# A gated cross-attention block: output projection by seven products over two head pairs, and a build-time planner for every queue

## The chip, the cores and the metric

The kernel runs on one core of a Trainium2 chip. A core has TensorE (PE in the profile; PEld is its loading of stationary operands), VectorE (DVE), ScalarE (ACT), GpSimd (POOL) and SyncE (SP), each with a queue of its own that it works off in order, and 16 DMA engines. Working memory is SBUF; matmul results go to PSUM, of which eight banks of 128 x 512 fp32 are used. The metric is device time in microseconds, the median of the runs.

## The reference

32 sequences of 64 tokens, width 512. With LN a layer norm without scale:

```
q = LN(x) Wq ; k = ctx Wk ; v = ctx Wv            32 heads of 128
P = softmax(q k^T / sqrt(128) + bias), keys masked per sequence
x1 = x + tanh(g0) * (P v) Wo
out = x1 + tanh(g1) * (LN(x1) W^T + b + LoRA(LN(x1)))   LoRA by sequence
```

All is fp32. Bias is 32 x 32 x 64 x 64, Wq, Wk, Wv are 512 x 4096, Wo is 4096 x 512, the last linear layer 512 x 512.

## The kernel before, in words

The tokens go through in two halves (`NPH` = 2) of 1024, eight tiles of 128 tokens (two sequences) each. Heads go in 16 pairs.

**Precision.** Large matmuls are split: an operand is rounded to a high part (`ACT` copy to `fp32r`) and a low part (a subtraction on DVE or POOL), and `mm3` (L93) issues high x high, high x low and low x high, three matmuls for one. Scores and values are plain fp32 matmuls of 64 columns (`ps` L862, `po` L1015).

**Seven products.** Keys, queries and values are made block by block, 2 x 2 blocks, by Strassen's scheme in Winograd's form: seven products instead of eight, from sums of weight blocks (`pair_blocks` L262, `weight_steps` L221) and of activation blocks (`sum_blocks` L149, `turned_blocks` L198). `unit` (L348) issues the seven and adds the results up on DVE (L350). Only the first two key pairs are done plainly, so that work starts early.

**Stages of one half.** Keys of 16 pairs, stored to memory (`kd`); values in four groups of eight heads, stored (`vd`); then attention, pair by pair: queries, scores, softmax, values, output projection. Layer norm of x is computed on rows and spread to columns through a small memory tile (`lnd`, `ln`). After both halves come the linear layer and LoRA (`ffn_chunk` L1339).

**Softmax.** For each head, DVE adds scores and bias (L864) and takes the row maximum (L866); POOL subtracts it (L867); ACT takes the exponential, 512 columns at once (L876); DVE sums rows (L886) and inverts; POOL multiplies (L889). For the value matmul the probabilities are needed keys by queries: DVE transposes 32 x 32 blocks (L900), and eight ACT copies of 32 x 256 (`copy` L894, L897) put the blocks into place in `pt`.

**Output projection.** `pv` (L1000) makes the context of a pair, features by tokens, split to `ch` and `cl` (L1019, L1020). `oproj` (L1063) multiplies each 128-token tile of it, as stationary operand, with that pair's rows of Wo, in six matmuls (two heads, three each) into `pa`, and DVE adds `pa` to the accumulator `acc` (L1068), which holds x and gets x1, tokens by features. `prep_o` (L1033) loads and splits the rows of Wo, in each half anew.

**What sets the order.** Instructions are issued by hand-written code. Side work is written as generators in a list `streams`; `beat` (L63) advances each by one step after each product, and `drain` finishes one. PSUM comes from one pool of eight rotating buffers.

**The end.** `ffn_turn` (L1292) normalizes and transposes a row tile of the second half and stores it to `xtd`; `ffn_load` (L1276) reads it back features by tokens in pieces of 128 bytes; `ffn_out` (L1319) makes the 16 output tiles. The first half's tiles are turned much earlier (`acc_turned` L681).

## Time and profile before

| | |
|---|---|
| median of 3 runs | 1475.67 us (1473.54 to 1477.26) |
| span of the profiled execution | 1476.7 us |
| matmul records / PE busy | 12006 / 1467.8 us |
| DVE, ACT, POOL busy | 945.4, 714.3, 1047.3 us |
| memory traffic | 259.38 MB, mean 176 GB/s |
| transfers on the SP queue | q1, 50.7% of the 16 DMA engines' time |

The profile is of one execution, whose span is the time between its first and its last instruction; no other time of that execution is given. A busy share is an average over stages. A line names the engine, the operation, the tile written and those read, the shape, the count, busy time and mean length; behind the second bar stands the idle time just before, and what ended it. Matmul records overlap, so the time of a matmul is read from how many of them fill a stretch. An fp32 matmul leaves two records.

### The profile page before, as it was taken

To read this page: it belongs to the slowest core of one execution; us is meant where nothing else is said; L and a number is where in the kernel's file an instruction comes from. 1 tells how busy PE (TensorE), PEld (TensorE's weight loads), DVE (VectorE), ACT (ScalarE), POOL (GpSimd) and SP (SyncE) were. 2 spreads that over 40 slices of the span, in tenths; PEclk is the share of its full clock that TensorE was granted. 3 is DMA by queue.
4 is the path that set the end of the run, shared out by engine and by line. 5 is a ranking of instruction groups with operands and counts; after the bars stand their busy time and mean duration, and the time that the engine had idled before them with its cause. 6 is when DMAs were issued, how large, how long until landed. Compare 5 with 4: busy or idle time off the path is not lost.

```text
span 1476.7 us, 31286 instructions
## 1 busy us (share of the span) xinstructions
PE 1467.8 (99%) x12006; PEld 1220.8 (83%) x12006; DVE 945.4 (64%) x1592; ACT 714.3 (48%) x1582; POOL 1047.3 (71%) x1156
## 2 busy tenths in 40 slices
PE   9999999999999999999999999999999999999999
PEld 7888888888888888887788888888888888888887
DVE  5675465367776677676479756435777567757774
ACT  5444233346645565566334423334655665466611
POOL 3999378969767576766989937897885767577520
PEclk9999999999999999999999999999999999999999
DMA  5754554375444355352385765446545254625554
GB/s 201 288 202 166 181 174 168 143 273 179 157 158 133 140 188 199 114 188 94 114 290 205 247 228 185 167 143 242 187 158 186 94 180 158 228 88 180 144 128 130
DMA packets 148344, 259.38 MB, mean 176 GB/s; under 512 B 44418, under 2 KB 78210, under 8 KB 144099
## 3 DMA queue, kind: packets, MB, share of 16 engines
q1 hardware_dynamic: 147906, 256.87, 50.7%
q8 instruction: 94, 1.54, 0.4%
q10 hardware_dynamic: 288, 0.52, 0.1%
q14 instruction: 56, 0.45, 0.1%
HBM read 179.74 MB, written 77.61 MB: 174 GB/s over the span
## 4 chain that ended last, share of the span: by engine, by line
PE 93%; POOL 3%; DMA 1%; issue 1%; DVE 1%; ACT 0%; POOLq 0%; DVEq 0%; ACTq 0%
PE pa L99 21%; PE pzv L99 6%; PE pvv L99 6%; PE pxv L99 6%; PE pxq L99 6%; PE pvk L99 5%; PE pzk L99 5%; PE pxk L99 5%; PE pvq L99 5%; PE pzq L99 5%; PE po L1015 4%; PE ps L862 4%; PE pf L99 3%; PE pyv L99 3%; PE pyk L99 3%; PE pyq L99 3%
## 5 line engine op out<-in xcount | busy, mean ns | idle before, releaser
L99 PE MATMUL pa<-wo,ch 128*128 128x512 f32 x896 | 278.9, 392 | 1.2 <-POOL sm L867 1.0
L897 ACT COPY pt<-tp 32x256 f32<-32x256 f32 x452 | 182.5, 404 | 68.9 <-DVE tp L900 59.6
L99 PEld LDWEIGHTS pa<-wo,ch 128*128 128x128 f32 x896 | 166.8, 188 | 37.4 <-POOL sm L867 1.3
L99 PE MATMUL pa<-wo,cl 128*128 128x512 f32 x448 | 174.1, 389 | 0.0
L1068 DVE TENSOR_TENSOR acc<-pa,acc 128x512 f32<-128x512 f32 x192 | 129.4, 681 | 53.5 <-PE pa L99 53.5
L816 POOL TENSOR_TENSOR sm<-sm,madd 128x512 f32<-128x512 f32 x60 | 77.1, 1293 | 89.0 <-DMA sm<-bias 88.7
L889 POOL TENSOR_TENSOR sm<-sm,r 128x512 f32<-128x512 f32 x64 | 66.8, 1044 | 73.0 <-DVE r L888 66.6
L350 DVE TENSOR_TENSOR vt<-pvv,vt 128x512 f32<-128x512 f32 x64 | 44.2, 691 | 100.6 <-PE pvv L99 100.6
L1020 DVE TENSOR_TENSOR cl<-po,ch 128x512 fp32r<-128x512 f32 x112 | 74.5, 689 | 50.1 <-ACT ch L1019 49.7
L99 PEld LDWEIGHTS pa<-wo,cl 128*128 128x128 f32 x448 | 84.1, 188 | 17.5
L867 POOL TENSOR_TENSOR sm<-sm,mx 128x512 f32<-128x512 f32 x64 | 66.9, 1048 | 41.2 <-DVE mx L866 41.2
L350 DVE TENSOR_TENSOR qT<-pvq,qT 128x512 f32<-128x512 f32 x64 | 44.1, 690 | 62.4 <-PE pvq L99 60.8
L372 ACT COPY vt<-pxv 128x512 f32<-128x512 f32 x32 | 18.8, 588 | 129.9 <-PE pxv L99 129.9
L876 ACT ACTIVATE sm<-sm 128x512 f32<-128x512 f32 x62 | 39.2, 633 | 77.4 <-POOL sm L867 77.4
L350 DVE TENSOR_TENSOR kT<-pvk,kT 128x512 f32<-128x512 f32 x60 | 41.1, 685 | 52.9 <-PE pvk L99 52.3
L90 POOL TENSOR_TENSOR wo<-rawo,wo 128x512 fp32r<-128x512 f32 x56 | 71.4, 1295 | 5.0 <-ACT wo L89 5.0
L1015 PEld LDWEIGHTS po<-pt,v 64*64 64x64 f32 x3840 | 59.6, 135 | 13.0 <-issue 11.4
L1019 ACT CAST ch<-po 128x512 fp32r<-128x512 f32 x112 | 62.9, 593 | 12.0 <-PE po L1015 11.9
L1015 PE MATMUL po<-pt,v 64*64 64x64 f32 x3840 | 64.0, 220 | 2.1 <-issue 1.7
L350 DVE TENSOR_TENSOR vt<-pzv,vt 128x512 f32<-128x512 f32 x64 | 44.2, 691 | 33.2 <-PE pzv L99 32.5
L862 PE MATMUL ps<-kB,qT 128*64 128x64 f32 x2048 | 65.0, 223 | 0.5 <-issue 0.4
L862 PEld LDWEIGHTS ps<-kB,qT 128*64 128x64 f32 x2048 | 62.0, 138 | 3.9 <-issue 2.2
(999 smaller groups left out, 3866.5 us busy)
## 6 DMA issues: line engine op xcount, KB each, us to landing
kd<-kT SPq DMA_DIRECT2D x64, 512.0 KB, 3.8
vd<-vt SPq DMA_DIRECT2D x128, 256.0 KB, 2.4
kB<-kd SPq DMA_DIRECT2D x32, 1024.0 KB, 10.2
v<-vd SPq DMA_DIRECT2D x32, 1024.0 KB, 8.0
rawq<-wq SPq DMA_DIRECT2D x32, 512.0 KB, 3.7
sm<-bias SPq DMA_DIRECT2D x64, 256.0 KB, 4.8
rawo<-wo SPq DMA_DIRECT2D x32, 512.0 KB, 3.7
rawk<-wk SPq DMA_DIRECT2D x31, 512.0 KB, 5.6
```

What stands on the lines that cost most here:

```text
L90: eng.tensor_tensor(lo, raw, hi.bitcast(F32), ALU.subtract)
L99: nc.tensor.matmul(ps, a, b, start=start and i == 0, stop=stop and i == len(todo) - 1, skip_group_check=True)
L350: nc.vector.tensor_tensor(o, ps, i, ALU.add)
L816: nc.gpsimd.tensor_tensor(t, t, masks[p][0], ALU.add)
L862: nc.tensor.matmul(ps[h * S:(h + 1) * S, t, :], qT[:, i, tok], kT[:, i, tok], start=True, stop=True)
L867: nc.gpsimd.tensor_tensor(s, s, mx.unsqueeze(2).to_broadcast([P, NT, S]), ALU.subtract)
L889: nc.gpsimd.tensor_tensor(t, t, r.unsqueeze(2).to_broadcast([P, NT, S]), ALU.mult)
L897: f(pts[n == NPR - 2][dst, i, :, qi * 32:(qi + 1) * 32], of[src, :, ki * 32:(ki + 1) * 32])
L1015: nc.tensor.matmul(ps[h][d:d + S, k, :], v[keys, t, i * P + d:i * P + d + S], pt[keys, i, t, :], start=True, stop=True)
L1019: nc.scalar.copy(o, ps[h])
L1020: nc.vector.tensor_tensor(l, ps[h], o.bitcast(F32), ALU.subtract)
L1068: nc.vector.tensor_tensor(acc[t], ps, acc[t], ALU.add)
```

## The change

The file is rewritten around a planner; the tiling into two halves, 16 pairs, and seven products for keys, queries and values stays.

1. *Planner.* Code no longer issues instructions; it records operations (`Plan.add`) with the engines that may run them, an assumed duration on each, and the tiles read and written. PE's operations keep the recorded order and carry the due times. [...] SBUF is cut into pages (41 of 4 KB, 26 of 2 KB per partition, and small ones) handed out at plan time; PSUM banks are named by the code. The instructions are then issued in the order of planned start.
2. *Output projection.* Wo's rows are formed once, in the first half's key and value stages (`out_forms`): four sums and seven splits per pair, stored to memory (`fd`), and read again for each half (`out_step`). The context of two heads in even and odd sequences gives the four blocks b11 to b22, from which `values` makes seven forms. A group of two pairs takes seven products by two column blocks, each of six matmuls with the Wo form as stationary operand. The accumulator becomes features by tokens.
3. *Softmax.* The negated scores are kept, DVE takes the row minimum, and ACT does the subtraction, exponential and row sum by eight activations of 64 columns, each with a bias by row. POOL's subtraction and DVE's row sum go. The eight copies per head become eight transfers per pair from `tp` to `pt`.
4. *Layer norm of x1 and the end.* Since `acc` is features by tokens, `turned` transposes it and stores it (`xbd`), `row_tile` reads rows in pieces of 128 bytes, and mean and deviation are spread back over columns. In the second half this stands between the last output product and the linear layer, beside the first half's eight tiles.
5. The token order within a half is even sequences, then odd ones; inputs and output are laid out accordingly.

Instructions, before and after: SP transfers 663 and 1557; POOL sums 256 wide 662 and 449, 512 wide 454 and 432; DVE sums 256 wide 28 and 417, 512 wide 942 and 904; split matmuls 512 wide 5810 and 5618.

```diff
-ORDER = ("p1", "p6", "p7", "p5", "p2", "p4", "p3")
+ORDER = ("p1", "p2", "p6", "p5", "p7", "p3", "p4")
+LAYER = {"p1": 0, "p2": 1, "p6": 0, "p5": 1, "p7": 0, "p3": 1, "p4": 0}
+MM = 0.2267
+PAGES = {"F4": 41, "F2": 26, "S": 30}
+CAPS = {"f": 10, "rk": 3, "rq": 3, "ro": 1, "fo": 4, "xs": 4, "xr": 4}
+LEAD = {"SP": 6.0, "ACTQ": 6.0}
+AHEAD = 45.0
...
+    def weight(o, s):
+        e, d = min(o.engs.items(), key=lambda x: x[1])
+        if e == "PE":
+            return d + 0.25
+        if e in ("SP", "ACTQ"):
+            return 2.2 + o.bytes / 2e5 + LEAD[e]
+        return d * 1.25 + 0.25
...
+                        o = None
+                        for c in sorted(ready[e], key=lambda o: (o.ls, o.n)):
+                            if c.port and e in ("DVE", "POOL") and port > now + 1e-9:
+                                continue
+                            if e == "DVE" and "POOL" in c.engs and c.ls > now + 12.0:
+                                continue
+                            if c.alloc and not can(c):
+                                continue
+                            o = c
+                            break
+                        if o is None:
+                            break
+                    self.start(o, e, now, free, pend, allocated, ready, kinds, short)
...
+def t_act(n):
+    return 0.218 + n * 0.000735
+def t_dve(n):
+    return 0.155 + n * 0.001042
+def t_pool(n):
+    return 0.185 + n * 0.002164
...
+    def unit(w, a, sl, dst, banks, nm):
+        A, B = {}, {}
+        def step(q):
+            first = q in ("p1", "p2", "p5")
+            if q == "p1":
+                A["t"] = bank(banks[0], f"pa{nm}")
+            if q in ("p2", "p5"):
+                B["t"] = bank(banks[1 if q == "p2" else -1], f"pb{nm}{q}")
+            ps = (B if LAYER[q] else A)["t"]
+            if sl is None:
+                terms = [(w[q][kt], a[q][kt]) for kt in range(2)]
+            else:
+                terms = [(tuple(b.then(lambda t: t[:, sl]) for b in a[q][kt]), w[q][kt]) for kt in range(2)]
+            product(ps, terms, first)
+            p = ps.at()
+            if q in ("p1", "p6", "p5", "p4"):
+                copy(dst[{"p1": (0, 0), "p6": (0, 1), "p5": (1, 1), "p4": (1, 0)}[q]], p, 512)
+            else:
+                d = dst[{"p2": (0, 0), "p7": (1, 1), "p3": (0, 1)}[q]]
+                tt(VEC, d, p, d, ALU.add, 512)
+        return [lambda q=q: step(q) for q in ORDER]
...
+    def out_forms(n):
+        late = pl.t_pe + 25.0
+        raw = page("F4", [P, 1024], F32, f"ro{n}")
+        dma(raw.at(), dwo.at(lambda t: t[n]), P * 4096, late=late - 15)
+        a11, a21, a12, a22 = [raw.at(lambda t, i=i: t[:, i * 256:(i + 1) * 256]) for i in range(4)]
+        forms = sums4((a11, a12, a21, a22), f"o{n}", late)
+        for k, q in enumerate(ORDER):
+            t = page("F2", [P, 2, 2, P], F32R, f"fo{n}{q}", 2)
+            jb = lambda v: v.rearrange("p (j b) -> p j b", j=2)
+            split(forms[q].then(jb), t.at(lambda t: t[:, :, 0, :], 0), t.at(lambda t: t[:, :, 1, :], 1), 256, late=late)
+            for j in range(2):
+                dma(fd[n // 2][j * 7 + k].at(lambda t: t[:, n % 2, :], n % 2),
+                    t.at(lambda t, j=j: t[:, j].rearrange("p h b -> p (h b)").bitcast(F32)), P * 1024, late=late)
...
-        def copy(f, n, i, of, h, qi, ki):
-            src = slice(h * 64 + qi * 32, h * 64 + qi * 32 + 32)
-            dst = slice(h * 64 + ki * 32, h * 64 + ki * 32 + 32)
-            f(pts[n == NPR - 2][dst, i, :, qi * 32:(qi + 1) * 32], of[src, :, ki * 32:(ki + 1) * 32])
+    def score(a, n, banks):
+        p = a.p
...
+            mn = page("S", [P, NT], F32, f"mn{p}_{n}_{i}")
+            pl.add({"DVE": 0.7}, [sa], [mn.at()],
+                   lambda e, s=s, mn=mn: e.tensor_reduce(mn.t, s.t.rearrange("p k t c -> p t k c"), AX.XY, ALU.min))
+            r = page("S", [P, NT], F32, f"r{p}_{n}_{i}")
+            def ex(e, s=s, mn=mn, r=r):
+                for t in range(NT):
+                    v = s.t[:, :, t, :]
+                    e.activation(v, v, AF.Exp, bias=mn.t[:, t:t + 1], scale=-1.0, accum_out=r.t[:, t:t + 1])
+            pl.add({"ACT": 2.2}, [sa, mn.at()], [sa, r.at()], ex)
+            def norm(e, r=r):
+                e.reciprocal(r.t, r.t)
+                e.tensor_tensor(r.t, r.t, rv.t, ALU.mult)
+            pl.add({"DVE": 0.36}, [r.at(), rv.at()], [r.at()], norm)
+            pl.add({"POOL": 1.05, "DVE": t_dve(512)}, [sa, r.at()], [sa],
+                   lambda e, s=s, r=r: e.tensor_tensor(s.t, s.t, r.t.unsqueeze(1).unsqueeze(3).to_broadcast([P, 2, NT, 32]), ALU.mult), port=True)
+            pl.add({"DVE": 0.7}, [sa], [tp.at(None, i)],
+                   lambda e, s=s, i=i: e.transpose(tp.t[:, :, i, :], s.t.rearrange("p k t c -> p k (t c)")))
+        pt = page("F4", [P, 2, 2, 256], F32, f"pt{p}_{n}", 8)
+        a.pt[n] = pt
+        for h in range(2):
+            for qi in range(2):
+                for ki in range(2):
+                    src, dst = [slice(h * 64 + b * 32, h * 64 + b * 32 + 32) for b in (qi, ki)]
+                    dma(pt.at(lambda t, d=dst, qi=qi: t[d, qi].rearrange("p i c -> p (i c)"), h * 4 + qi * 2 + ki),
+                        tp.at(lambda t, s=src, ki=ki: t[s, ki].rearrange("p i c -> p (i c)")), 65536)
...
+        flat = lambda t: t.rearrange("p t s -> p (t s)")
+        b11, b12, b21, b22 = [ps[i][h].at(flat) for i in range(2) for h in range(2)]
+        g = {}
+        nm = f"g{p}_{n}"
+        def form(q, src, engs):
+            t = page("F4", [P, 2, 512], F32R, f"{nm}{q}", 2)
+            hi, lo = t.at(lambda t: t[:, 0], 0), t.at(lambda t: t[:, 1], 1)
+            split(src, hi, lo, 512, engs)
+            g[q] = (hi, lo)
+        def temp(k):
+            return page("F2", [P, 512], F32, f"{nm}{k}").at()
+        form("p1", b11, VEC)
+        c12 = temp("c")
+        copy(c12, b12, 512)
+        t1, t2, t3, t4 = [temp(f"t{k}") for k in (1, 2, 3, 4)]
+        tt(VEC, t1, c12, b11, ALU.subtract, 512)
+        form("p2", b21, VEC)
+        tt(VEC, t2, b22, t1, ALU.subtract, 512)
+        form("p6", t2, BOTH)
+        form("p5", t1, BOTH)
+        tt(VEC, t3, b22, c12, ALU.subtract, 512)
+        form("p7", t3, BOTH)
+        form("p3", b22, VEC)
+        tt(VEC, t4, b21, t2, ALU.subtract, 512)
+        form("p4", t4, BOTH)
+        a.g[n] = g
...
-        def o_terms(n, t):
-            h, lo = ctx_of(n)
-            w = b["o", n]
-            sl = slice(t * P, (t + 1) * P)
-            return [((h[:, i, sl], lo[:, i, sl]),
-                     (w[:, 0, i * 512:(i + 1) * 512], w[:, 1, i * 512:(i + 1) * 512])) for i in heads_of(n)]
-        def oproj(n, ts=range(NT)):
-            drain(ob.get(n))
-            for t in ts:
-                ps = psum(f"pa{p}_{n}_{t}")
-                mm3(ps, o_terms(n, t), last=(2, 5) if n == 0 and t == 0 else ())
-                nc.vector.tensor_tensor(acc[t], ps, acc[t], ALU.add)
-                beat()
+    def out_step(a, m, j, k, banks, last=False):
+        q = ORDER[k]
+        t = page("F2", [P, 2, 2, P], F32, f"f{a.p}_{m}_{j}{q}")
+        dma(t.at(lambda t: t.rearrange("p n h b -> p (n h b)")),
+            fd[m // 2][j * 7 + k].at(lambda t: t.rearrange("p n c -> p (n c)")), P * 2048)
+        terms = [(tuple(t.at(lambda t, n=n, hl=hl: t[:, n, hl, :].bitcast(F32R)) for hl in range(2)), a.g[m + n][q]) for n in range(2)]
+        key = "A" if not LAYER[q] else "B"
+        if q in ("p1", "p2", "p5"):
+            a.ps[key, j] = bank(banks[LAYER[q]], f"pc{a.p}_{m}_{j}{q}")
+        ps = a.ps[key, j]
+        product(ps, terms, q in ("p1", "p2", "p5"))
+        d = a.acc[{"p1": (0, 0), "p2": (0, 0), "p6": (0, 1), "p5": (1, 1), "p7": (1, 1), "p3": (0, 1), "p4": (1, 0)}[q]][j]
+        tt(VEC, d, ps.at(), d, ALU.add, 512)
...
+        for c in range(2, NPR // 2):
+            us = query_unit(a, 2 * c, xq, qb(0)) 
+            later = lambda: query_unit(a, 2 * c + 1, xq, qb(1))
+            os = out_steps(a, 2 * c - 4)
+            us[0]()
+            us[1]()
+            for k in range(14):
+                os[k]()
+                if k + 2 == 7:
+                    us += later()
+                if k + 2 < 14:
+                    us[k + 2]()
+                if k == 1:
+                    score(a, 2 * c - 1, sb(1))
+                if k == 7:
+                    score(a, 2 * c, sb(0))
+                if k == 10:
+                    values(a, 2 * c - 2, B4)
+            values(a, 2 * c - 1, B4)
+        after_q()
+        os = out_steps(a, NPR - 4, True)
+        score(a, NPR - 1, (0, 1))
+        for k in range(14):
+            os[k]()
+            if k == 7:
+                values(a, NPR - 2, B4)
+        values(a, NPR - 1, B4)
+        finish()
...
+    def turned(a):
+        for h in (1, 0):
+            for i in range(2):
+                for j in range(2):
+                    ft = 2 * i + j
+                    v = a.acc[i, h][j]
+                    t = page("F2", [P, 512], F32, f"xt{a.p}_{ft}{h}")
+                    pl.add({"DVE": 0.7}, [v], [t.at()], lambda e, v=v, t=t: e.transpose(t.t, v()), late=pl.t_pe + 5.0)
+                    dma(xbd[a.p].at(lambda d, ft=ft, h=h: d[h, ft], h * KT + ft), t.at(), P * 2048, late=pl.t_pe + 8.0)
+                    if a.p == 0:
+                        dma(xtd.at(lambda d, ft=ft, h=h: d[h, ft], h * KT + ft), v, P * 2048, late=pl.t_pe + 8.0)
+    def row_tile(p, t):
+        h, u = t // 4, t % 4
+        b = page("F2", [P, D], F32, f"{'xr' if p == 0 else 'xz'}_{t}", 4)
+        for c in range(4):
+            dma(b.at(lambda v, c=c: v[c * 32:(c + 1) * 32].rearrange("p (f k) -> p f k", k=32), c),
+                xbd[p].at(lambda d, c=c: d[h].rearrange("f (a q) w -> q (f a) w", a=4)[:, :, (4 * u + c) * 32:(4 * u + c + 1) * 32],
+                          *range(h * KT, (h + 1) * KT)), 32 * 2048, ("SP", "ACTQ")[c % 2] if p else "SP", late=pl.t_pe + t)
+        return b.at()
+    def row_moments(p, h):
+        n = NT // 2
+        mv = page("S", [P, n, 2], F32, f"mvr{p}{h}", n)
+        rows = []
+        for u in range(n):
+            t = h * n + u
+            r = row_tile(p, t)
+            moments(r, mv, u, f"r{p}_{t}", None if p else pl.t_pe + 20.0)
+            rows.append(r)
+            if p == 0:
+                dma(x1d.at(lambda d, t=t: d[t], t), r, P * 2048, late=pl.t_pe + 40.0)
+        return rows, spread(mv, deviation(mv, n, f"r{p}{h}"), n, f"r{p}{h}")[0]
...
+                turned(a)
+                made = {h: row_moments(1, h) for h in (1, 0)}
+                for t in range(NT):
+                    tile0(t)
+                for h in (1, 0):
+                    rows, spr = made[h]
+                    src1 = [a.acc[kt // 2, h][kt % 2] for kt in range(KT)]
+                    normalize([src1], [spr])
+                    act = ffn_act(1, h, src1)
+                    low = ffn_low(1, h, act, h)
+                    for u in range(4):
+                        t = h * 4 + u
+                        ffn_tile(1, t, act, low, rows[u], 4 + u if t != 3 else 2, 2 if t == 3 else 1)
...
+    seq = pl.schedule()
+    for o in seq:
+        for b in o.alloc:
+            if b.cls in PAGES:
+                b.t = pool.tile(b.shape, b.dt, tag=f"{b.slot[0]}_{b.slot[1]}", name=b.name)
+            elif b.cls:
+                b.t = psp.tile(b.shape, b.dt, tag=b.cls, name=b.name)
+        o.emit(ENG[o.eng])
```

## The prediction

> **What bounds the kernel now.** I read the busy shares first. TensorE (PE) has a matmul in flight for 99% of the span, at full granted clock.
>
> ```profile
> span 1476.7 us, 31286 instructions
> PE 1467.8 (99%) x12006; PEld 1220.8 (83%) x12006; DVE 945.4 (64%) x1592; ACT 714.3 (48%) x1582; POOL 1047.3 (71%) x1156
> ...
> PEclk9999999999999999999999999999999999999999
> ```
>
> Second, the chain that ended last, by engine and line, and then in order of time (start, length, what). It is PE nearly throughout, and the output projection `pa` is its largest item.
>
> ```profile
> PE 93%; POOL 3%; DMA 1%; issue 1%; DVE 1%; ACT 0%; POOLq 0%; DVEq 0%; ACTq 0%
> ```
> ```profile
> 359.23 2.02 PE po L1015 x128
> 361.25 1.59 PE pxq L99 x6
> 362.84 1.36 PE pyq L99 x6
> ...
> 371.00 3.88 PE ps L862 x128
> 374.88 11.11 PE pa L99 x48
> ...
> 407.28 10.88 PE pa L99 x48
> ```
>
> A 512-wide split-precision matmul costs 10.88/48 = 0.2267 us. The first group after an fp32 block (`ps`, `po`) costs 0.23 us more: 11.11 against 10.88, 1.59 against 1.36. These are the durations that matter, as matmul records of 390 ns overlap.
>
> Third, the groups of instructions, for prices (busy, mean ns, then idle before).
>
> ```profile
> L897 ACT COPY pt<-tp 32x256 f32<-32x256 f32 x452 | 182.5, 404 | 68.9 <-DVE tp L900 59.6
> L1068 DVE TENSOR_TENSOR acc<-pa,acc 128x512 f32<-128x512 f32 x192 | 129.4, 681 | 53.5 <-PE pa L99 53.5
> L867 POOL TENSOR_TENSOR sm<-sm,mx 128x512 f32<-128x512 f32 x64 | 66.9, 1048 | 41.2 <-DVE mx L866 41.2
> L1019 ACT CAST ch<-po 128x512 fp32r<-128x512 f32 x112 | 62.9, 593 | 12.0 <-PE po L1015 11.9
> L876 ACT ACTIVATE sm<-sm 128x512 f32<-128x512 f32 x62 | 39.2, 633 | 77.4 <-POOL sm L867 77.4
> ```
>
> Fourth, DVE in order of time in the second key stage: where POOL runs a sum of two SBUF tiles, DVE's own two-tile sum takes 1.25 us instead of 0.69. The two engines take turns. Back to back, a 512-wide DVE operation starts every 0.61 us; POOL's start every 0.70 us (256 wide).
>
> ```profile
> 777.38 0.69 DVE L350 TENSOR_TENSOR kT<-pzk,kT 128x512 f32<-128x512 f32 x1
> 777.99 0.16 DVE L117 TENSOR_SCALAR yx<-vx 128x8 int32<-128x8 int32 x1
> 778.06 1.25 DVE L186 TENSOR_TENSOR vs<-wvr_0b,vs 128x512 f32<-128x512 f32 x1
> ```
>
> Fifth, the first key and value stages by window (busy PE, PEld, DVE, ACT, POOL, then clock, DMA share, GB/s), and the transfers.
>
> ```profile
> 33.00:166.00 133.00, 133.00 (x589) 110.12 (x587) 78.47 (x128) 55.15 (x132) 110.41 (x143) 1.00 0.59 209
> 166.00:320.00 154.00, 154.00 (x681) 127.53 (x680) 78.85 (x117) 53.66 (x101) 124.53 (x103) 1.00 0.51 180
> ```
> ```profile
> xt<-xtd SPq DMA_DIRECT2D x64, 64.0 KB, 2.4
> ...
> ln<-lnd SPq DMA_DIRECT2D x8, 256.0 KB, 3.7
> ```
> ```profile
> 1383.37 9.64 SPq L1281 DMA_DIRECT2D xt<-xtd  x16
> ```
>
> **The change part by part.** The sum is made against the profiled span, 1476.7 us; the runs' median, 1475.67, lies 1.0 lower, inside the runs' spread.
>
> *Products.* Before: 2 halves x 16 pairs x 8 tiles x 6 = 1536 matmuls. After: 16 groups of two pairs x 7 products x 2 column blocks x 6 = 1344. 192 fewer at 0.2267 = -43.5 us, all on the bound engine. [...]
>
> *More changes between fp32 and split matmuls.* Scores and values now stand singly between products. Counted in the instruction orders, split matmuls follow an fp32 block 62 times, before 40. 22 x 0.22 = +4.8 (bounds 0, if it hides, and 5.1).
>
> *ACT.* Gone: 484 block copies x 0.404 = -196 and 64 exponentials x 0.633 = -41. Added: 512 exponentials 64 wide, with a bias by row and a row sum. No such row exists; between the 256- and 512-wide copies the slope is 0.74 ns per element, so 0.264 each at least, and I bound it above by the 256-wide copy, 0.404: +135 to +207; I take 0.27, the length being nearest to the extrapolation. Context forms: 256 copies instead of 128, +76; output-weight forms about +6. ACT then has some 695 to 767 us, about half the span: no bound. [...]
>
> *DVE and POOL in total.* By the instruction orders DVE gains 389 sums of 256 (0.413) and loses 64 row sums (0.673), 28 small transposes (0.432) and 38 sums of 512: 945+161-43-12-26 = about 1025 us. POOL loses 213 of 256 (0.75) and 22 of 512: about 874. Neither is a bound on average.
>
> *The shared turn of DVE and POOL, first key and value stages.* To the 14x11 sums of 256 for key weights and 88 of 512 for value weights come 16x11 of 256 for the output forms. All on POOL that is 330x0.70 + 88x1.25 = 341 us, and PE has 287: DVE must take a part, at 0.35 and 0.61, in turn with POOL. Along the new instruction order, priced so, the two together have 268 us of two-tile work in the 272 us of matmul from 30 us on: 98%. Before, these stages had POOL 235 of 287. With the remainders so near the limit, PE will wait here and there. Bounds: 0 (DVE takes more) and 20 (the ends of seven stretches of 40 us each late by 3). I take +4, nearest to before, where 100 us at such a share cost PE nothing.
>
> *Value blocks and their banks.* All value blocks now use the same four PSUM banks, and within an iteration the second follows the first after four products, 5.4 us, plus 1.0 for its first head. To free the banks DVE does seven 512-wide forms and one or two `acc` additions, 8.5 x 0.61 = 5.2, after the first copy (0.59) and some 0.25 of signalling at each end: 6.3 to 7.3 against 6.4. Fourteen such places: 0 to 21, and I take 0.35 each, +5. Before, eight rotating buffers hid this.
>
> *Probabilities by transfers.* 8 copies per head go; 8 transfers of 64 KB per pair come (256), on SP. From score to probabilities: 0.68+0.69+2.2+0.4+1.05+0.69 per head, two heads partly overlapped, 8 x 0.36 of issue and 2.4 to land: about 14 us. The nearest value block lies 12 products of 2.7 us behind its score: 33. Cost nothing; the cover must shrink by 19 to show.
>
> *SP and DMA.* SP issues 1557 transfers instead of 663, at 0.33 to 0.37 (0.60 for 128-byte pieces): about 570 us, below half. Traffic, counted: 258 to 363 MB. The page has 50.7% of the DMA engines for 259 MB; the mean becomes about 72%. In the first key and value stages: 209x133 + 180x154 = 55.5 MB, plus 16 output weights (8.4) and 224 forms written (29.4) = 93.3 MB. By before's share (2.83 us per MB) that is 264 of 287 us. Close, but covered: 0; end of range +35, as a rival below.
>
> *The tail.* The accumulators now hold features by tokens, so layer norm of the second half needs a turn through memory. Its cover: 8 first-half tiles x 14 x 0.2267 = 25.4, plus the last two products, 2.7: 28.1. The path: addition 0.94, transpose 0.70, store 2.75, eight gathers per queue 4.8 and landing 2.4, statistics 0.86, fifteen small operations 3.0, store 2.1, read back 4.05, eight normalizing sums and four remainders 12x0.61 + 0.5 = 7.8, and signals between some twenty steps 3: 32.4. DVE also does first-half evictions and the other group's statistics between, some 5. 37 - 28 = +9. Bounds: 0 (POOL shares the sums and queues run ahead) and 18 (gathers land twice as late). Before, PE ran through this stage without a break, so it is all new.
>
> Sum: 1476.7 - 43.5 + 4.8 + 4 + 5 + 9 = 1456.0, on the scale of the median 1455.
>
> **The rivals.**
> - *All covered.* Turns, banks and tail hide: 1476.7 - 43.5 + 4.8 - 1 = 1437. For it: ACT, DVE and POOL have room on average. Against: the tail's path has no row that would shorten it.
> - *DMA sets the first stages' pace (slower).* The forms' 128 KB writes stand in the queue ahead of weights that PE needs. The best slice of the page moved 290 GB/s; at that pace 93.3 MB take 322 us, 35 more than PE: 1490. It decides from 303 GB/s down, where the 21 us of gain are gone. For it: 92% share. Against: half of the forms are needed only much later and can wait.
> - *Value blocks wait for banks by more.* At 1.5 us in each of fourteen places: 1455 + 16 = 1471, no change. For it: DVE executes in order, and an `acc` addition that waits for its product holds the forms behind it. Against: the order was laid out with durations that the rows bear out (0.69, 1.29, 0.2267).
>
> That the products stay as many is excluded by the instruction order (5618 wide matmuls for 5810).
>
> **How the numbers follow.** Forecast case, 1445 to 1470: 0.52. All covered or better, below 1445: 0.23. Banks or tail at their upper ends, 1471 to 1480: 0.08. DMA pace or an order that does not hold on the chip, above: 0.17. Range 1437 (all covered) to 1484 (half of the DMA case). No-change means within 0.3%, about 4.4 us, what this measurement can tell. Faster 0.75, same 0.08, slower 0.17.
>
> **What would show it.** Right: matmul groups of 0.2267 as before, PE idle 15 to 25 us more, half of it before the second half's `pt` near the end. Wrong by the turns: PE waiting for POOL or DVE forms of weights before 320 us. Wrong by banks: `po` waiting for DVE. Wrong by DMA: key or value weights waiting for `wk`, `wv`, at a DMA share of 0.9. The whole fails if order and chip drift apart: then PE waits everywhere, a little each time.

## The result, and the profile after

The changed kernel takes 1564.66 us (median of four runs, 1558.32 to 1566.69) beside 1476.47 of the kernel before in the same comparison: ratio 1.0595, 95% interval 1.0569 to 1.0621. It is 88 us slower, 81 us above the end of my range.

The page of after: span, busy time by engine, the granted clock in 40 slices, and the shares of the chain that ended last.

```profile
span 1564.9 us, 33409 instructions
PE 1477.3 (94%) x11814; PEld 1199.7 (77%) x11814; DVE 1055.6 (67%) x1857; ACT 822.0 (53%) x2422; POOL 903.5 (58%) x891
PEclk9999999999999999999999999999999999999998
PE 67%; DMA 15%; DVE 5%; issue 4%; ACT 4%; POOL 3%; SPq 2%; ACTq 0%; DVEq 0%; POOLq 0%
```

PE is idle for 88 us (1564.9 - 1477.3; before: 9), and the chain, which was 93% PE, now passes through transfers for 15% of the span. No engine is full: DVE, ACT and POOL have a third to a half free. So PE does not wait for a full engine; it waits in many places for something late. The clock adds to it: the records have 13 windows at half clock, 68 us in all. PE was busy for 55 us of them, which at half rate is a loss of some 28 us, an estimate from these two numbers. Before, there was no such window.

The chain in order of time, in the second attention stage (start, length, what):

```profile
1305.35 8.70 DMA rq<-wq
...
1314.43 0.41 ACT wq_12p L352
...
1315.98 1.51 ACT sm L739 x9
1317.49 0.48 ACT qT L352
...
1318.02 2.93 PE pbq_11p L377 x6
1320.94 3.09 PE po L776 x128
```

PE at the same place, with its idle time and what ended it in brackets:

```profile
1318.02 2.93 PE L377 MATMUL pbq_11p<-q1p,wq_11p 128*128 128x512 f32 x6 [4.24 <-ACT qT L352]
```

This is the pattern of the attention stages. The raw query weights of a later pair (`rq`) take 8.70 us from issue to landing. ScalarE stands in its queue at their cast (`wq_12p`), behind it come an exponential block and then the copy `qT` that empties a PSUM bank (below, such a copy or addition is called an eviction). PE waits 4.24 us for that copy, and its next six matmuls take 2.93 us instead of 1.36: the clock has been halved. The same picture stands at 472, 1252 and 1358 us, and at 1200 us with a transfer `pt<-tp` of 6.88 us named in the load's place.

What SP issues just then (start, length, operation, count):

```profile
1305.35 0.42 SPq L366 DMA_DIRECT2D rq<-wq  x1
1307.18 7.40 SPq L366 DMA_DIRECT2D pt<-tp  x8
1314.68 0.53 SPq L366 DMA_DIRECT2D kB<-kd  x1
```

Eight placing transfers (`pt<-tp`, which put the probabilities into place) keep SP for 7.4 us; the next keys (`kB`) stand behind them. Some 4.5 us of that are the eight issues, 0.51 to 0.60 us each. The longest gaps are waits for one of the eight semaphores that tell of landings, of which each transfer needs one: the seventh was issued 0.02 us after the landing that freed its semaphore, and the eighth, at 1314.07, 0.02 us after the landing of `rq` itself. And the exponentials, in the groups:

```profile
L739 ACT ACTIVATE sm<-sm,mn 128x64 f32<-128x64 f32 x512 | 170.6, 335 | 50.2 <-DVE mn L733 46.3
L739 ACT ACTIVATION_READ_ACCUMULATOR sm<-sm,mn 128x1 f32 x512 | 96.2, 188 | 0.0
```

Each one is two instructions, and on ScalarE one exponential starts every 0.33 us: 2.65 us per head. The planner assumed 2.2, and I had 8 x 0.27.

The windows of the first key stage, the first value stage and the second value stage (length, then busy time of PE, PEld, DVE, ACT, POOL, clock, DMA share, GB/s):

```profile
27.80:164.10 136.30, 134.90 (x590) 109.91 (x589) 97.44 (x166) 85.00 (x211) 101.77 (x121) 1.00 0.91 305
164.10:333.40 169.30, 157.97 (x673) 127.14 (x671) 102.87 (x196) 83.89 (x177) 108.61 (x84) 0.98 0.89 290
...
914.10:1067.20 153.10, 153.10 (x673) 126.20 (x672) 58.79 (x91) 70.12 (x129) 136.83 (x114) 1.00 0.62 199
```

The two value stages have the same 673 matmul records; the first, which makes output-weight forms beside them, is 16 us longer.

All later readings go by stages, from the first product of a stage to the first of the next, read from the matmul records (us). "Linear" goes from the first product of the linear layer's low-rank part to the end of the last matmul. The head of a column is the number of the run, as told below. Each run but 1, 2 and 9 was planned anew with its edit, so that its order of instructions differs too.

| stage | after | 3 | 4 | 7 | 9 | 10 | 11 | 13 | 17 |
|---|---|---|---|---|---|---|---|---|---|
| keys 1 | 136.3 | 135.0 | 134.0 | 134.6 | 134.3 | 133.7 | 133.7 | 134.3 | 135.0 |
| values 1 | 169.4 | 168.7 | 170.1 | 167.6 | 168.7 | 152.3 | 158.9 | 168.6 | 152.6 |
| attention 1 | 394.0 | 370.9 | 378.0 | 370.9 | 388.4 | 391.8 | 368.0 | 378.2 | 379.9 |
| keys 2 | 186.7 | 191.6 | 175.5 | 179.8 | 186.8 | 189.8 | 178.1 | 178.2 | 178.0 |
| values 2 | 153.2 | 153.5 | 153.3 | 152.9 | 153.2 | 152.3 | 152.3 | 153.5 | 153.9 |
| attention 2 | 398.1 | 363.7 | 375.0 | 368.0 | 386.6 | 397.7 | 361.5 | 366.8 | 366.0 |
| linear | 96.3 | 94.5 | 95.0 | 91.2 | 94.2 | 93.5 | 78.0 | 90.7 | 88.0 |
| median of the runs | 1564.7 | 1510.3 | 1516.1 | 1496.9 | 1541.5 | 1542.5 | 1464.8 | 1498.2 | 1486.7 |

### The profile page after: what moved, and what is told of

Read it like the earlier page. It is cut to its first block, busy times and chain, and to the rows that moved or that the text cites. A ratio compares the mean times of both kernels' runs of the same rounds, so it can differ in the third digit from the quotient of the medians.

```text
span 1564.9 us, 33409 instructions
## 1 busy us (share of the span) xinstructions
PE 1477.3 (94%) x11814; PEld 1199.7 (77%) x11814; DVE 1055.6 (67%) x1857; ACT 822.0 (53%) x2422; POOL 903.5 (58%) x891
## 4 chain that ended last, share of the span: by engine, by line
PE 67%; DMA 15%; DVE 5%; issue 4%; ACT 4%; POOL 3%; SPq 2%; ACTq 0%; DVEq 0%; POOLq 0%
PE paq L377 9%; PE pc_0p L377 8%; PE pc_1p L377 7%; PE pak L377 7%; PE pav L377 7%; PE po L776 4%; PE ps L727 3%; DMA rq<-wq 2%; ACT sm L739 2%; SPq L366 2%; DMA vd<-vt 2%; PE pbv_0p L377 1%; PE pf L377 1%; PE pbv_1p L377 1%; PE pbv_3p L377 1%
## 5 line engine op out<-in xcount | busy, mean ns | idle before, releaser
L739 ACT ACTIVATE sm<-sm,mn 128x64 f32<-128x64 f32 x512 | 170.6, 335 | 50.2 <-DVE mn L733 46.3
L739 ACT ACTIVATION_READ_ACCUMULATOR sm<-sm,mn 128x1 f32 x512 | 96.2, 188 | 0.0
L352 ACT COPY qT<-paq 128x512 f32<-128x512 f32 x96 | 55.5, 582 | 65.2 <-PE paq L377 64.5
L352 ACT COPY vt<-pav 128x512 f32<-128x512 f32 x96 | 55.5, 586 | 57.5 <-PE pav L377 31.1
L357 DVE TENSOR_TENSOR acc<-pc_1p,acc 128x512 f32<-128x512 f32 x112 | 75.3, 678 | 6.7 <-PE pc_1p L377 6.5
L357 DVE TENSOR_TENSOR acc<-pc_0p,acc 128x512 f32<-128x512 f32 x112 | 75.4, 674 | 2.8 <-PE pc_0p L377 2.7
L357 DVE TENSOR_TENSOR kT<-pak,kT 128x512 f32<-128x512 f32 x30 | 20.6, 685 | 83.1 <-PE pak L377 66.8
L352 ACT COPY kT<-pak 128x512 f32<-128x512 f32 x90 | 52.4, 584 | 37.2 <-PE pak L377 29.0
L719 POOL TENSOR_TENSOR sm<-sm,mf 128x512 f32<-128x512 f32 x40 | 53.2, 1342 | 31.8 <-DMA sm<-bias 21.0
L749 DVE STREAM_TRANSPOSE tp<-sm 128x512 f32<-128x512 f32 x64 | 44.1, 698 | 20.8 <-PE ps L727 14.1
L377 PE MATMUL pf<-wf,fa 128*128 128x512 f32 (+1 forms) x204 | 47.9, 384 | 2.5 <-DVE ot L1012 2.5
```

Source lines behind the costliest of these rows:

```text
L352: pl.add({"ACT": t_act(n)}, [i], [o], lambda e: e.copy(o(), i()), late=late)
L357: lambda e: e.tensor_tensor(o(), a(), b().bitcast(F32) if cast else b(), f), port="POOL" in engs or engs == ("SDVE",), late=late)
L377: nc.tensor.matmul(ps, a(), b(), start=start and i == 0, stop=i == len(todo) - 1, skip_group_check=True)
L719: lambda e, s=s: e.tensor_tensor(s.t, s.t, mf.t, ALU.add), port=True)
L739: e.activation(v, v, AF.Exp, bias=mn.t[:, t:t + 1], scale=-1.0, accum_out=r.t[:, t:t + 1])
L749: lambda e, s=s, i=i: e.transpose(tp.t[:, :, i, :], s.t.rearrange("p k t c -> p k (t c)")))
```

## The experiments

In the code of the edits below, `...` and `..` stand for lines and arguments that are not shown.

### Runs 1 to 4: bytes, exponentials, number of transfers, order

Theories: A, too many bytes, so loads land late; B, the exponentials are too long; C, too many transfers; D, only the planner's numbers are off.

**Run 1**, a quarter of the bytes of every form, same transfers and order:

```diff
-dma(fd[..][:, n % 2, :], t[:, j], ...)        # P * 1024 bytes
+dma(fd[..][:, n % 2, 0:64], t[:, j, 0, 0:64], ...)
-dma(t, fd[m // 2][j * 7 + k], P * 2048)
+dma(t[:, 0, 0, :], fd[m // 2][j * 7 + k][:, :, 0:64], P * 2048)
```

> Edit: of every output-weight form only a quarter is stored and read back (64 instead of 256 columns per row and form), and the product reads that quarter four times. The number of transfers, all pages, all other instructions and the planned order stay as they are; 66 of 364 MB go, which at 71.5% of 1564.9 us for 360 MB (3.1 us of all 16 DMA engines per MB) is some 205 us of DMA time. The output projection's numbers are therefore not the reference's. Theory A (loads land later than the order assumes, because the DMA engines have too much to carry; PE then waits behind ScalarE's queue, and its clock is cut after the wait): most of the loss goes, about half of the 87.6 us of PE idle time and half of the 34 us that the cut clock costs, so 1565 - 60 = 1505 (1480 to 1525). Theory B (ScalarE's exponentials are longer than planned) and theory C (the number of transfers on SP, not their bytes): 1550 or more.

Measured: 1536.7 us, 28 less. A asked for 60. Removing 66 of 364 MB leaves more than two thirds of the loss; these bytes are a part, not the whole cause.

**Run 2**, one exponential per head:

```diff
-for t in range(NT):
-    e.activation(v, v, AF.Exp, bias=mn.t[:, t:t + 1], scale=-1.0, accum_out=r.t[:, t:t + 1])
+e.activation(s.t, s.t, AF.Exp, bias=mn.t[:, 0:1], scale=-1.0)
+e.copy(r.t, mn.t)
```

> Edit: one exponential of 512 columns per head instead of eight of 64 with a row sum each; the row minimum of the first tile stands in for all eight, and the minima stand in for the row sums, so the softmax's numbers are not the reference's. The planned order stays (the planner is still told 2.2 us). ScalarE's part of a head falls from 2.65 us (eight starts 0.33 apart) to about 0.8, 64 x 1.85 = 118 us of its 822. Theory B (exponentials take 2.65 instead of 2.2, evictions queue behind them): 1510 to 1530. Theory A (late loads): ScalarE's waits for loads stay, 1545 or more. Theory C: 1550 or more.

Measured: 1542.9 us, 22 less, at 116 us less of ACT. Between B and A: the length of the exponentials counts although ACT was only 53% busy. That it does so because they stand ahead of evictions is read from the chain above; no run moves the evictions alone.

**Run 3**, one placing transfer per pair:

```diff
-for h, qi, ki in ...: dma(pt[d, qi], tp[s, ki], 65536)
+dma(pt, tp, 524288)
```

> Edit: the probabilities of a pair go from tp to pt in one transfer of 128 rows instead of eight of 32 rows (no block is put in another place, so the values' numbers are not the reference's). Same bytes; 224 transfers fewer, and SP has 224 x 0.6 = 134 us less to issue; order planned anew with that. Theory C (SP's queue: 0.59 us for each of these issues, and issues that stand until one of eight transfers in flight has landed, 268 of 1581 in the profile): 1500 to 1520. Theory A (bytes): 1545 or more. Theory B: 1555 or more.

Measured: 1510.3 us, 54 less. The attention stages fall by 23 and 34 us, the second key stage grows by 5, the others stay within 2. It is the largest gain of one edit, and inside theory C's range. The order was planned anew, so the 54 us are the transfers' and the new order's together.

**Run 4**, three planner numbers:

```diff
-pl.add({"ACT": 2.2}, ...)            ; SP issue 0.36                    ; o.end = dma + 0.4
+pl.add({"ACT": 2.75}, ...)           ; SP issue 0.44, 0.62 for 64 KB    ; o.end = dma + 1.4
```

> Edit: three numbers of the planner alone, after the profile: exponentials 2.75 us per head (2.2), issue on SP 0.44 us and 0.62 for a 64 KB transfer (0.36), and each landing 1.0 us later. The chip has the same instructions in another order. Theory D (only the order is wrong, the engines could do it): 1490 to 1510. Theory A: loads can't be had sooner in the stages where the DMA engines are at 0.86 to 0.99, only the in-order waits of ScalarE in the attention stages go: 1525 to 1550.

Measured: 1516.1 us, 48.5 less, with the work of the kernel kept (47 operations move from POOL to DVE) and its whole output computed: between D and A, nearer to D. Attention falls by 16 and 23 us, the second key stage by 11. So the order, fixed when the kernel is built (`schedule` gives each engine the ready operation whose latest start comes first), is worth nearly as much as run 3: on engines that work in order, an order made for transfers that land sooner and exponentials that end sooner puts the waiting instruction ahead of the one that PE needs. Which of the three numbers counts was not tried singly.

### Runs 7 to 9: one loss or two, and what is dear in the placing

**Run 7** is runs 3 and 4 together.

> Edit: the one transfer per pair of the third run and the measured planner numbers of the fourth together. Alone they gave 54 and 48 us. If both work on the same loss in the attention stages (late transfers behind the eight placing transfers), most of the gain overlaps there and only the second key stage's 16 us of the fourth run add: 1490 to 1500. If they are separate losses, 1565 - 54 - 48 = 1463.

Measured: 1496.9 us. The gains overlap: 54 and 48 give 68, not 102. The attention stages (370.9, 368.0) lie near run 3's, the second key stage (179.8) nearer to run 4's. With run 4's numbers the seven transfers of a pair are worth 19 us (1516.1 to 1496.9), not 54: much of what they cost, they cost through an order that was wrong for them.

**Run 8** places the blocks by ScalarE again, as the kernel before did: `copy(pt[d, qi], tp[s, ki], 512)` in place of the eight transfers, with run 4's numbers.

> Edit: one part undone, with the right result: the eight transfers of a pair from tp to pt become eight copies of 32 x 512 on ScalarE, and the planner has the measured numbers. 256 transfers go; ScalarE gets 256 x 0.5 = 129 us (822 to 950 of some 1500), as in the kernel before. If the transfers' turn on SP was the loss, it ends near the one-transfer run, 1495 to 1510; if ScalarE, whose waits for loads hold up the evictions, was near its limit, it gains nothing over the fourth run's 1516.

Measured: 1525.6 us, 9.5 more than run 4. The profile has ACT at 970.9 us and new waits of PE for `acc` (10.5 us, twelve times) and for `pt` (7.1). Undoing this part of the change does not pay within the rest of it.

**Run 9** keeps eight transfers, of which one carries all bytes:

```diff
-dma(pt[d, qi], tp[s, ki], 65536)                        # eight times
+k == 0: dma_start(pt, tp)   else: dma_start(scr[k * 32:k * 32 + 32], tp[s, 0, 0, 0:4])
```

> Edit: of a pair's eight transfers from tp to pt the first moves all 128 rows (512 KB), and the other seven move 16 bytes from each of 32 rows to memory that nobody reads. Number of transfers, their place in SP's queue and the planned order are those of the kernel after; the bytes are those of the one-transfer run. No block is put in another place, so the values' numbers are not the reference's. Theory C1 (each transfer costs a turn of SP's queue, 0.59 us, and one of eight places in flight, whatever it carries): 1550 or more, the attention stages at 390 to 400 us as in the kernel after (394.0, 398.1). Theory C2 (what is dear is the form, 64 KB from 32 rows, which the DMA engines work off more slowly than one transfer of 128 rows): 1515 to 1530, the attention stages near the one-transfer run's 370.9 and 363.7.

Measured: 1541.5 us, between C2 and C1, nearer to C1. Of run 3's 54 us, 23 go with the shape of 64 KB from 32 rows (a longer issue included: 0.59 us each on SP, the small ones 0.42), and 31 come only when the seven transfers go and the planner makes another order. How the 31 us divide between SP's turn, the places in flight and the order is not shown. In the profile after, 268 of 1581 transfers were issued within 0.3 us of the landing that freed their landing semaphore, of which there are eight; before, 6 of 665.

### Runs 5, 10 and 14 to 18: the first value stage

**Run 5** leaves out the stores of the forms of 14 pairs (`for j in range(2 if n < 2 else 0)`).

> Edit: the forms of 14 of the 16 output-weight pairs are computed as before but not stored (196 of 224 transfers of 128 KB, 25.7 of 29.4 MB go), and each group of two pairs reads the first group's forms; bytes and transfers of the reads, and all sums, stay. The output projection's numbers are not the reference's. In the profile after, the first value stage took 169.4 us, with 11.4 us of PE idle and 6.8 us at half clock, and the second, without forms, 153.2. Theory A1 (the stores stand in SP's queue ahead of value blocks and weights): the first value stage falls to 153 to 157, the run to 1548 (1543 to 1553). Rival (DVE and POOL, whose shared turn I had priced at 4 us, set this stage's pace; the forms' sums stay): the stage stays at 165 or more, the run at 1560 or more.

Measured: 1563.5 us; the stage 163.5. Theory A1 does not hold: 6 of 16 us of the stage, and the run as a whole gains 1 us, less than its runs differ by.

**Run 10** leaves out the making of these forms as well (`out_forms` for two pairs only).

> Edit: as in the run without the stores, but the forms of 14 of 16 output-weight pairs are not made at all in the first key and value stages: no loads of Wo, no sums, no splits there (14 x 4 sums and 14 x 7 remainders of 256 on DVE or POOL, 98 casts). The output projection's numbers are not the reference's. The first value stage had 169.4 us in the kernel after, 163.5 without the stores, and the second one, which has no forms, 153.2. Theory (the shared turn of DVE and POOL and ScalarE's casts for the forms hold back value weights and blocks): 153 to 157. Rival (the stage is slow for what surrounds it, such as the layer norm of x and the loads of the attention stage ahead): 162 or more.

Measured: 1542.5 us, the stage 152.3 with no idle time. The forms cost the first value stage 17 us, by their loads, sums, splits and stores together.

**Runs 14 and 15** keep all work and make the forms of pairs 9 to 15 in the first attention stage; run 15 also tells the planner 300 GB/s instead of 330. They build on run 13 (below).

```diff
-in value_group: if p == 0 and k in (2, 12, 22): out_forms(pos)
+in attend:      if a.p == 0 and k in (0, 6) and a.nf < NPR: out_forms(a.nf)
```

> Edit, right result: the run before, and the output-weight forms of pairs 9 to 15 are made in the first attention stage instead of the first value stage. If it is those forms that make the first value stage long (169 us, 152.3 without any), it falls to 153 to 156 and the first attention stage, whose POOL is at 45%, takes them for some 5 us: 1495 to 1500. If they only move the loss: 1505 or more.

> Edit, right result: the run before, with the planner's transfer rate at 300 GB/s instead of 330 (slices of the profile after moved 270 to 350 GB/s where the DMA engines were at 0.86 to 0.99). If planned order and chip still drift apart by the transfers' rate: 5 to 10 us less than the run before, 1487 to 1493. If the order is now good enough: within 4 us of it.

Measured: 1508.2 and 1505.3 us; the stage 168.4 and 169.5. The first expectation's theory failed: with all but the last few operations of the forms out of it, the stage was as long as with them. Run 15 lies within 4 us of run 14, so the planner's rate is not what is missing. The instructions of DVE in run 14's first value stage, in order of time (start, length, engine, line, operation, tiles, shape):

```profile
234.29 18.34 DVE L568 TENSOR_SCALAR vx<-mvx 128x8 f32<-128x8 f32 x1
252.66 0.17 DVE L569 TENSOR_SCALAR yx<-vx 128x8 int32<-128x8 int32 x1
```
```profile
294.24 15.26 DVE L640 CAST stf<-sti 128x4 f32<-128x4 int32 x1
```

and POOL's at the same time:

```profile
247.49 5.12 POOL L357 TENSOR_TENSOR wv_3p<-vs,wv_3p 128x512 fp32r<-128x512 f32 x4
252.68 2.56 POOL L357 TENSOR_TENSOR vs<-rv,vs 128x512 f32<-128x512 f32 x2
```

An addition on eight columns kept DVE for 18.34 us, where the next operation of the same size took 0.17, and a conversion of four columns for 15.26. POOL ran sums without a pause from before 234 to 252.60, and DVE came free at 252.63, in POOL's first pause, of 0.08 us. The second was held until 309.51, POOL's last sum ended at 309.48. DVE's evictions stood behind: 8.1 of PE's 11.2 us of waits in this stage come right after the two. The kernel after has the same at 812.46 us, in the second key stage, where POOL runs normalizing and weight sums without a pause until 820.97:

```profile
812.46 8.54 DVE L568 TENSOR_SCALAR vr<-mvr 128x4 f32<-128x4 f32 x1
```

**Runs 16, 17 and 18** take these small operations off DVE: the deviation to POOL, the adapters' to the start. 16 is the kernel after with that edit alone, 17 is run 14 with it, 18 is run 13 with it.

```diff
-small(VEC, [V], [W], lambda e: e.tensor_scalar(w.t, v.t, -0.5, None, ALU.mult))
+small(GPS, [V], [W], lambda e: e.tensor_scalar(w.t, v.t, -0.5, None, ALU.mult))
...
             xc = first_keys()
+            adapters(60.0)
...
-                if p == 0:
-                    adapters(pl.t_pe + 100.0)
+                pass
```

> Edit to the kernel after, right result: the nine small operations of the deviation (four or eight columns; the last of each of its three rounds as two) go from DVE to POOL, and the adapters' small operations to the start of the kernel. In the profile after, one of them, 128 x 4, kept DVE from 812.46 to 821.00 us, as long as POOL ran sums without a pause, and two of TensorE's waits of the second key stage (3.24 at 809, 2.86 at 823) lie around it. Theory (a small DVE operation that reads SBUF alone gets its turn only when POOL pauses, and the evictions behind it wait): none is held any more, the second key stage falls from 186.7 to 178 to 181, the run to 1557 to 1561. Rival (the held operation costs nothing, TensorE's waits come from ScalarE's loads): 185 or more, the run within 3 us of 1565.

> The same edit to the run with late forms (1508), where DVE was held for 18.34 us at 234.3 by the deviation, 15.26 at 294.2 by a copy of four columns, and 10.59 at 766.7. Theory: the first value stage falls from 168.4 to 154 to 158, the second key stage from 179.8 to 172 to 177, the run to 1487 to 1495. Rival (the forms' sums themselves, not the held operations, are the loss): 165 or more, 1502 or more.

> The same edit to the run with four transfers (1498), whose forms are made in the first value stage as in the kernel after and in which no small operation was held for more than 3 us there (DMA engines at 0.9 to 0.94 from 210 to 345 us). Theory that the stores and loads of that stage are its loss: the first value stage stays at 165 to 169, the run at 1494 to 1500. If held operations were its loss too: below 160, 1486 to 1490.

Measured: 1562.9, 1486.7 and 1499.8 us. Run 17 is as expected: its first value stage takes 152.6 us with no idle time, 16 less than run 14's, and everything is computed. Run 18 is too: where no small operation was held, moving them gains nothing (1499.8 beside 1498.2) and the stage stays at 168.7, so there the forms are the loss. A held operation costs PE time only if something PE needs stands behind it: in run 17's stage a 512-wide DVE sum was held for 12.31 us at 289.9, and PE did not wait. Run 16's expectation failed: the second key stage fell only to 184.4. Its profile has another small copy held for 5.35 us at 798 and a wait of 4.97 us for ScalarE's `kT` at 816; what makes the kernel after's second key stage long is not settled beyond run 4, whose order alone takes 11 us off it.

Run 17's windows of the first value stage and the two attention stages:

```profile
163.30:315.90 152.60, 152.60 (x673) 126.11 (x672) 69.10 (x99) 72.56 (x136) 132.43 (x120) 1.00 0.69 221
315.90:695.80 379.90, 366.00 (x4340) 299.38 (x4339) 335.05 (x588) 242.76 (x863) 230.46 (x241) 1.00 0.82 271
...
1027.70:1393.70 366.00, 361.83 (x4333) 297.92 (x4331) 312.93 (x551) 226.07 (x808) 182.80 (x183) 1.00 0.74 235
```

### Runs 6 and 12: the end

**Run 6** leaves out the second half's turn through memory (`turned(a)` and `row_moments(1, h)`; other tiles stand in).

> Edit: the second half's layer norm after the output projection is left out: no transposes, stores, gathers of row tiles, statistics and no spread back; the normalizing sums take other tiles of the same size as operands, and the residual rows are the first half's, so half of the output is not the reference's. In the profile after, the last stage (first linear-layer product to the end) took 71.9 us, 13.0 of them idle, with 13.7 at half clock. Theory T (the turn through memory is longer than its cover): the stage falls by 13 + 7 = 20 us to some 52, the run to 1545 (1541 to 1549). Rival (what the last products wait for is not the turn but DVE's evictions and splits, which stay): 65 or more, the run above 1556.

Measured: 1544.0 us, 20.6 less; the last stage, from the first linear-layer product to the end of the last, falls from 71.9 to 54.8. As expected: the turn costs 17 us.

**Run 12** fills PE's wait there with matmuls that nobody reads, on run 4's kernel:

```diff
+hot = bank(3, "hot")
+pl.add({"PE": 36 * MM}, [ah, wh], [hot.at()], lambda e: [
+    nc.tensor.matmul(hot.t, ah()[:, 0:P], wh(), start=True, stop=True) for _ in range(36)])
```

> Edit: the fourth run's kernel (measured planner numbers, right result), and ahead of the second half's linear layer 36 matmuls of 512 columns into a PSUM bank that nobody reads, 36 x 0.2267 = 8.2 us, which fits into the 9.5 us that TensorE waits there. In the fourth run 13.7 us at half clock followed this wait. If the clock is cut because TensorE paused: no cut there, the last stage 69.4 - 6.8 = 62.6 us (61 to 65), the run 1516 - 7 = 1509. If the cut has another cause or the extra matmuls only delay: 69 to 78, the run 1516 to 1524.

Measured: 1513.7 us (run 4: 1516.1). PE at that place, run 4 first, then run 12:

```profile
1474.59 0.80 PE L977 MATMUL pt<-fa,a 128*128 128x512 f32 x1 [9.51 <-ACT fa L352]
```
```profile
1468.25 8.32 PE L1171 MATMUL hot<-wf,fa 128*128 128x512 f32 x36
1477.24 0.49 PE L977 MATMUL pt<-fa,a 128*128 128x512 f32 x1 [0.67 <-ACT fa L352]
1478.94 0.50 PE L978 MATMUL pt<-fa,a 128*128 128x512 f32 x1 [1.21 <-DVE fa L357]
```

The cause of the clock is shown: without the pause there is no half-clock window (`pt` 0.49 us instead of 0.80, 0 us at half clock in the stage instead of 13.7). The price is not what I had taken, half of the window: the stage takes 68.9 us beside 69.4. Half of run 4's window, from 1467.34 to 1480.99, lay over the pause itself, so that PE lost some 3 us by it, not 7; and in run 12 the products wait 4.0 us, most of it for the splits `fa` on ACT and DVE.

### Runs 11 and 13: what is left, and what is left with everything computed

**Run 11** joins runs 3, 4, 6 and 10.

> Edit: the edits together: one transfer per pair, the measured planner numbers, no turn at the end, no forms in the first stages. If the named causes are all of the loss, it ends at the one-transfer run with measured numbers, 1497, less 20 (the turn and its clock) and less 10 to 14 (the first value stage): 1463 to 1468, which is what the forecast of 1455 should have come to. If losses move elsewhere when one is taken away: 1480 or more.

Measured: 1464.8 us, ratio 0.9928 (0.9908 to 0.9948). The named parts hold the loss. Without any forms its first value stage still took 158.9 us, beside run 10's 152.3: the cast of four columns held DVE for 12.83 us at 285.18, and PE waited 3.3 us for the eviction behind it. The page of run 11:

```profile
span 1461.8 us, 32267 instructions
PE 1435.7 (98%) x11814; PEld 1183.4 (81%) x11814; DVE 945.7 (65%) x1594; ACT 791.2 (54%) x2324; POOL 939.3 (64%) x946
```

**Run 13** halves the placing transfers and computes everything: DVE transposes a second time, straight into `pt`, and only the blocks off the diagonal are moved (run 4's numbers).

```diff
+pl.add({"DVE": 0.7}, [sa], [pt.at()], lambda e: e.transpose(pt.t[:, :, i, :], s.t...))
-for h, qi, ki: dma(pt[d, qi], tp[s, ki], 65536)
+for h, qi: ki = 1 - qi; dma(pt[d, qi], tp[s, ki], 65536)
```

> Edit, right result: DVE writes the transposed probabilities to tp and once more straight to pt, whose blocks on the diagonal are then in place; only the four blocks off the diagonal go by transfers of 64 KB from 32 rows. 128 transfers and 8.4 of 16.8 MB go, 64 transposes come (64 x 0.61 = 39 us of DVE, at 71%). Measured planner numbers, as in the fourth run (1516). If the number of placing transfers is the main loss: half of the way from the fourth run to the one-transfer run with the same planner (1497), 1503 to 1510. If the form is: also about half, and the two can't be told apart here. If DVE's extra transposes, behind which its evictions wait, take it back: 1515 or more.

Measured: 1498.2 us (ratio 1.0152, 1.0131 to 1.0173), 18 less than run 4, below the 1503 to 1510 expected, and close to run 7's 1496.9: halving the placing transfers gives nearly all of it, and the 64 more transposes on DVE cost nothing that shows. Their number and their bytes halve together here, and can't be told apart. With run 14's and run 17's edits on top it is 1486.7 us, ratio 1.0059 (1.0030 to 1.0089): 78 of the 88 us are back, with everything computed. No version that computes everything beat the kernel before.

## Why the prediction was wrong

- **Products, -43.5, and fp32 changes, +4.8: right.** 192 matmuls went (12006 to 11814), and groups of six still take 1.36 us. Run 11 has 1461.8 us of span, 22 of them idle between matmuls and 2 lost at half clock: 1438 us are left, against 1437 in the rival "all covered", which still holds PE's 9 us of idle time before.
- **Probabilities by transfers, "Cost nothing": the step that failed.** I compared the path from score to probabilities (14 us) with its cover (33). That path was in time, or nearly: of PE's waits before value blocks the profile puts 1.6 us down to `pt`, and for another 8.0 it names no cause.

```profile
PE po L776 <- issue: 8.0, 6, 3.6
PE po L776 <- DMA pt<-tp: 1.6, 2, 1.4
```

What the transfers cost is others' time, by their turn on SP (7.4 us for eight), their places in flight and their shape: the weights and keys behind and beside them land late. That is 54 us with the planner's first numbers (run 3), and still 19 with run 4's (run 7).

- **ACT, "no bound", also failed.** Busy share was the wrong question. The exponentials took 2.65 us a head (I had 2.2), an instruction for the row sum that I had not counted included, and evictions stood behind them and behind casts that waited for loads: 22 us (run 2). The sum for ACT also left out evictions: `unit` now copies four of its seven results by ACT, where two were copied before, 376 copies of keys, queries and values instead of 188, about 110 us more. So ACT was busy for 822 us, above my 767, and more of what PE waits for stands in its queue. The copies of queries, two groups of before, then the larger of the two after:

```profile
L355 ACT COPY qT<-pxq 128x512 f32<-128x512 f32 x32 | 19.2, 600 | 17.2 <-PE pxq L99 16.6 <-ACT x0p L177 0.3 <-ACT x1p L177 0.3
L372 ACT COPY qT<-pxq 128x512 f32<-128x512 f32 x32 | 18.7, 583 | 1.6 <-PE pxq L99 1.3
...
L352 ACT COPY qT<-paq 128x512 f32<-128x512 f32 x96 | 55.5, 582 | 65.2 <-PE paq L377 64.5
```

- **"The whole fails if order and chip drift apart: then PE waits everywhere, a little each time."** I had named it and given it, with the DMA case, 0.17. It is what happened: run 4 gets 48 us by order alone. I let the planner's durations pass because those of DVE, POOL and PE agreed with the rows; for its exponentials there was no row, its transfers I held against none, and I did not price a stall there.
- **The shared turn, +4 (0 to 20): mis-sized.** The forms cost the first value stage 17 us (run 10), near my upper bound, at DVE 102.87 and POOL 108.61 of 169 us. Neither was full, so the turn as I had priced it, a sum of busy time, is not what cost it; nor was a DVE operation held there for over 3 us. 6 us go with the stores alone (run 5). PE's waits of this stage are for evictions of value blocks, most on ScalarE, and these copies stood 14.6 us, in five waits, until earlier stores `vd<-vt` had landed. How the other 11 us divide between the forms' loads, sums and casts is not shown.
- **DMA in the first stages, "covered: 0": right for the keys, not for the values.** 0.91 and 0.89 of the DMA engines were used, as worked out, and the key stage lost 1.4 us of PE time. The rival "DMA sets the first stages' pace" holds for a part of the value stage: taking 25.7 MB out (run 5) shortened it by 6 us, though the run gained only 1.
- **Banks, +5: not seen.** The profile after puts no wait of `po` down to DVE, though the 8.0 us without a name could hide one. The 0.25 us of signalling in that sum was an assumption: in the profile before, an idle DVE starts at 408.68, 0.04 us after the record of the last `pa` matmul ends and 0.20 after the next matmul starts.
- **The tail, +9 (0 to 18): mis-sized.** 17 us (run 6), at the upper bound.
- **The clock: missing.** Some 28 us, by the estimate above, are lost by PE at half clock after pauses. No term stood for it: the records of before have no window at half clock within the span, and PE's longest pause there is 1.73 us (before a value block at 666.64). In the profile after, nine pauses lasted over 3 us, up to 9.57, and eight of them were followed by a window at half clock; the counts over all profiles stand below. Each window of the after profile halves PE's rate for 3.4 to 13.7 us, as far as PE has work in it, which a sum of waits has to carry beside them. That all of it could be had back is not shown: run 12 took one window away and gained 0.5 us in its stage.
- **The upper end of the range, 1484,** is not "half of the DMA case" by the prediction's own numbers: 1455 and half of 35 make 1472. The measured time lies above both.

So the mechanism of the gain was right, and the sum was wrong by its method: it priced each part against its own cover, on engines a third free, when the parts share in-order queues. The losses of the runs do not add up to 88 us; they overlap, as run 7 shows, and only run 11 takes them all together.

## What to carry to other kernels

When a fixed order replaces a tolerant one, price the order: take the two or three durations that nobody has measured, lengthen each by a quarter (run 4's exponentials and issues were longer by about that), and ask which eviction then stands behind which load. A small transfer or a small vector operation has no small price if it stands in a queue ahead of what the bound engine needs (here 0.59 us of SP for 64 KB, and up to 18.34 us of DVE for eight columns): count issues and places in flight, not bytes alone, and ask which neighbour can hold the operation. And price the clock after a pause of PE: here half clock followed 98 of 104 pauses over 3 us; in run 12 taking one window away gained only 0.5 us of its stage, where the next products then waited 4.0 us for other engines.

## What the runs showed of the hardware that I had not expected

- **The clock after a pause.** In the 19 profiles of this kernel and its variants, 98 of 104 pauses of PE over 3 us were followed within 7 us by a window at half clock, 48 of 75 of 2 to 3 us, and 6 of 81 of 1 to 1.5 us. The windows last 3.41, 6.83, 10.2 or 13.7 us, multiples of one length; in the profile after, eight last 3.41, four 6.83 and one 13.65. In run 12, filling the pause with matmuls that nobody reads prevented it.
- **A held vector operation.** DVE operations of four or eight columns that read and write SBUF took 8.54, 15.26 and 18.34 us while POOL ran two-tile sums without a pause; behind the 8.54 and the 18.34 the next operation of the same size took 0.17. The wait was not for one instruction: DVE waited through every POOL instruction of the streak, 15 of them each time in run 14, and came in at POOL's first pause. What holds DVE meanwhile is not shown.
- **The row sum of an activation.** `accum_out` adds an instruction of 188 ns; activations of 64 columns with it start every 0.33 us, where I had 0.27.
- **A transfer of 64 KB from 32 rows** keeps SP for 0.59 us (median of 256), one of 128 rows for 0.33 to 0.44 (medians of the tensors with 64 or more such transfers in the kernel after). One transfer of 128 rows in place of eight of 32, 224 transfers less in the attention stages, gave 54 us with the planner's first numbers (run 3) and 19 with the measured ones (run 7).
